# Reordering one step of a cross-attention block: seven-product sums between two transposes, low exponentials and the first norm ahead of the key copies

## The chip, the core and the metric

The kernel runs on one core of one Trainium2 chip. The metric is the time of one execution on the device in microseconds; the median of three runs stands for a kernel. A profiled execution gives in addition a trace of every engine, from which all rows in this document are copied.

The core has a matrix engine (TensorE, PE in the rows; its weight loads are PEld), a vector engine (VectorE, DVE), a scalar engine (ScalarE, ACT), a general engine (GpSimd, POOL) and SyncE (SP), whose queue only starts transfers here. Each engine carries out its own instructions in the order in which they were written, and waits on semaphores for the others.

## The reference

128 independent sequences of 128 positions with 256 features go through one block of cross-attention and a feed-forward network, all in float32:

```python
q = heads(x @ Wq + bq); k = heads(ctx @ Wk + bk); v = heads(ctx @ Wv + bv)   # 16 heads of 16
scores = where(j < i, q @ k.T / sqrt(16), -1e30)                            # strictly causal
attn = softmax(scores); attn[:, :, 0, :] = 0
x1 = layer_norm(x + (attn @ v) @ Wo + bo, ln1_g, ln1_b)
out = layer_norm(x1 + relu(x1 @ W1 + b1) @ W2 + b2, ln2_g, ln2_b)           # W1: 256 x 1024
```

## The kernel before

Two sequences make a pair, and 64 pairs `p` go through a software pipeline. From pair 5 on, one call `step(p)` does one turn of it: it works on five pairs at once, each in another stage. The first five pairs have functions of their own, and so have the last two (`behind`). The queues of all five engines are put under a manual schedule: an engine's order is the order of the calls in the code, and this order, written by hand, is what the change touches.

What one `step(p)` holds, by stages:

- **Attention weights of pair p.** `scores_both` computes the scores on TensorE into PSUM banks 0 to 3 (the high 64 rows of queries, 128 keys, "high") and 4 to 7 (the low 64 rows, 64 keys, "low"). VectorE adds the causal mask (line 378 for low, line 729 for high) and takes negative maxima (lines 733, 740). ScalarE makes the exponentials head by head with the maximum as bias (`exponential_by_head`, line 748: 16 instructions for high, reading PSUM, 16 for low, reading the masked copy in SBUF). VectorE sums them and takes the reciprocal (`sums`, lines 409 and 410, twice for high and once for low), and GpSimd scales by it (line 411). VectorE transposes the result in blocks of 32 (`turn`, line 424, three times), and SyncE brings the blocks to their partitions with 16 transfers (`bring`, line 439) as `pT`.
- **Projections.** Queries and keys of pair p + 1 and values of pair p, on TensorE (lines 257 and 289), copied out of PSUM by ScalarE (`queries` 268, `keys` 279, `values_out` 299 and 304). Tokens and context of pair p + 2 are transposed by VectorE (`tokens`, line 243). `keys` uses bank 0, `queries` bank 4, `values` bank 1.
- **Attention output of pair p - 2.** `weigh` multiplies `pT` by the values (lines 471 and 481) into bank 7, `context` copies it (493, ScalarE), `attention_out` applies Wo (500, bank 5), VectorE adds the input and takes statistics (526, 513, 514), GpSimd turns them into a scale and a shift (520, 521, 565), ScalarE applies them (`norm1`, line 542, two instructions), which gives `x1`. `turn_x1` transposes it: VectorE in blocks (651), then SyncE out to DRAM and back (lines 235 and 238, five transfers).
- **Feed-forward layer of pairs p - 3 and p - 4.** `hidden(p - 3)` multiplies by W1 (line 687, 32 matmuls in banks 2, 3, 4, 0) with ScalarE's ReLU behind it (693, eight instructions). `second_by_seven(p - 4)` does the product with W2 as seven products of half size (line 780) into bank 6 (`py`) and bank 7 (`pz`), from sums of `hT` that GpSimd makes (`combine_hidden`, 766 to 769). `sum_of_seven(p - 4)` puts the seven together with `x1b`, in five adds on VectorE (four of line 808 and one of line 816) into `t2`, followed by statistics (513, 514).
- **End of pair p - 5.** `norm2` on ScalarE (line 579, two instructions), `finish` on GpSimd (585, 586), `store` on SyncE (594). `residual1(p - 3)` on GpSimd (554, 557) makes `x1b` from `x1`.

Tiles are reused in turn: `t2` has two buffers, `x1`, `t1`, `x1T` two, `hT` and `hS` one; scores, their transposes and `pT` share four ("wide"). The whole order of TensorE in a step is `weigh`, scores, queries, `attention_out`, keys, values, the seven products, `hidden`.

Of the kernel before, what the change touches and what calls it, by code (L numbers as in the profile page):

```python
# [19 lines left out]
def tile_cross_attention_block(  # L20
# [26 lines left out]
    H = 16  # L47
# [225 lines left out]
    def keys(p):  # L273
        st = states[p]
        st["kT"] = proj.tile([P, KC, 2, TP], F32, tag="kT", name=f"kT_{p}")
        pk = project(wk, st["cT"], at_bank(0, f"pk_{p}") if p > 3 else bank(f"pk_{p}"))
        for m in range(KC):
            for e in range(2):
                nc.scalar.activation(  # L279
                    st["kT"][:, m, e, :], pk[:, m * TP : (m + 1) * TP], AF.Identity,  # L280
                    bias=bkh[:, m, e : e + 1], scale=half[:, e : e + 1],
                )

    def values(p):
        st = states[p]
        pv = st["pv"] = at_bank(1, f"pv_{p}") if p > 3 else bank(f"pv_{p}")
        for s in range(2):
            for k in range(KC):
                nc.tensor.matmul(  # L289
                    pv[:, s * D : (s + 1) * D], st["cT"][:, k, s * P : (s + 1) * P], wv[:, k, :],  # L290
                    start=(k == 0), stop=(k == KC - 1),
                )

    def values_out(p):
        st = states[p]
        pv = st.pop("pv")
        st["vz"], st["vd"] = vzs[p % 2], vds[p % 2]
        for s in range(2):
            nc.scalar.copy(  # L299
                st["vz"][:, s, :, 0:4:3, :],  # L300
                pv[:, s * D : (s + 1) * D].rearrange("p (r e d) -> p r e d", e=2, d=DK),
            )
        for e in range(2):
            nc.scalar.copy(  # L304
                st["vd"][e * HP : (e + 1) * HP, :, :, e, :].rearrange("p s r d -> p (s r) d"),
                pv[:HP].rearrange("p (u e d) -> p u e d", e=2, d=DK)[:, :, e, :],
            )
# [93 lines left out]
    def sums(p, hi, part):  # L401

        st = states[p]
        sm = st["sm", hi]
        n = sm.shape[2]
        su = small.tile([P, H], F32, tag=f"su{hi}", name=f"su{hi}_{p}_{part.start}")
        rs = small.tile([P, H], F32, tag=f"rs{hi}", name=f"rs{hi}_{p}_{part.start}")
        su, rs = su[:, part], rs[:, part]
        nc.vector.tensor_reduce(su, sm[:, part, :], AX.X, ALU.add)  # L409
        nc.vector.reciprocal(rs, su)  # L410
        nc.gpsimd.tensor_tensor(  # L411
            sm[:, part, :], sm[:, part, :],
            rs[:, :, None].to_broadcast([P, part.stop - part.start, n]), ALU.mult,
        )
# [119 lines left out]
    def norm1(p):  # L534

        st = states[p]
        x1 = st["x1"] = ffn.tile([P, 2, D], F32, tag="x1", name=f"x1_{p}")
        t1, mv, sd = st.pop("t1"), st.pop(("mv", 1)), st.pop(("sd", 1))
        for s in range(2):
            if p != 1:  # L540

                nc.scalar.activation(  # L542
                    x1[:, s], t1[:, s], AF.Identity, bias=st["nb", 1][:, s], scale=sd[:, s]
                )
                continue
            nc.vector.tensor_scalar(
                x1[:, s], t1[:, s], mv[:, s, 0:1], sd[:, s], ALU.subtract, ALU.mult
            )

    def residual1(p):  # L550

        st = states[p]
        x1b = st["x1b"] = ffn.tile([P, 2, D], F32, tag="x1b", name=f"x1b_{p}", bufs=3)
        nc.gpsimd.tensor_tensor(
            x1b, st["x1"], g1_r[:, None, :].to_broadcast([P, 2, D]), ALU.mult
        )
        nc.gpsimd.tensor_tensor(
            x1b, x1b, be1b_r[:, None, :].to_broadcast([P, 2, D]), ALU.add
        )

    def shift(p, i):
        st = states[p]
        nb = st["nb", i] = small.tile([P, 2, 1], F32, tag=f"nb{i}", name=f"nb{i}_{p}")
        for s in range(2):
            nc.gpsimd.tensor_scalar(
                nb[:, s], st["mv", i][:, s, 0:1], st["sd", i][:, s], -1.0, ALU.mult, ALU.mult
            )
# [7 lines left out]
    def norm2(p):  # L575
        st = states[p]
        t2, sd, nb = st["t2"], st["sd", 2], st["nb", 2]
        for s in range(2):
            nc.scalar.activation(  # L579
                t2[:, s], t2[:, s], AF.Identity, bias=nb[:, s], scale=sd[:, s]  # L580
            )
# [160 lines left out]
    def exponential_by_head(p, hi, heads):  # L742

        st = states[p]
        sm, nmx = st["sm", hi], st["nmx", hi]
        for h in heads:
            src = st["sps", 1][h // 4][:, h % 4 * P : h % 4 * P + P] if hi else sm[:, h, :]
            nc.scalar.activation(sm[:, h, :], src, AF.Exp, bias=nmx[:, h : h + 1], scale=1.0)  # L748
# [359 lines left out]
    def step(p):  # L1108
        last = p == NP - 1
        weigh(p - 2)  # L1110
        context(p - 2)
        scores_both(p)
        if p > 6:
            combine_hidden(p - 4, POOL_ALONE)
        if p == 5:
            second_sum(1)
            finish(0)
            store(0)
        add_bo(p - 1)
        load_ahead(p)  # L1120
        mask(p, 0, B)
        mask_high(p, A)
        exponential_by_head(p, 1, ONES)
        mask_high(p, B)
        exponential_by_head(p, 1, TWOS)
        mask(p, 0, A)
        low_maximum(p)
        if p > 5:
            norm2(p - 5)
        if not last:  # L1130
            queries(p + 1)
        exponential_by_head(p, 0, range(H))
        attention_out(p - 2)
        attention_sum(p - 2)
        attention_stats(p - 2)
        shift(p - 2, 1)
        if not last:
            keys(p + 1)
        values(p)
        values_out(p)  # L1140
        sums(p, 1, ONE)
        sums(p, 1, TWO)
        sums(p, 0, ALL)
        residual1(p - 3)
        if p > 6:
            second_by_seven(p - 4)
        elif p == 6:
            second_half(2, 1)
        norm1(p - 2)
        hidden(p - 3, range(FC // 2 if p == 5 else 0, FC))  # L1150
        if p == 5:
            second_half(2, 0)
        if p + 2 < NP:
            tokens(p + 2, "x")
            tokens(p + 2, "c")
        turn_x1(p - 2)
        turn(p, 1, 0)
        turn(p, 1, 1)
        turn(p, 0, 0)
        bring(p, nc.sync, LATE_FIRST)  # L1160
        if p > 5:
            finish(p - 5)
            store(p - 5)
        if p > 6:
            sum_of_seven(p - 4)
        stats(p - 4, states[p - 4]["t2"], 2)
        scale_and_shift(p - 4)

# [3 lines left out]
    for p in range(5, NP):  # L1172
        step(p)
# [23 lines left out]
    p = NP - 1  # L1197
# [71 lines left out]
```

## Time and profile before

| | |
|---|---|
| median of three runs | 1646.58 us (1645.24 to 1646.58) |
| the profiled execution's own time | 1644.42 us |
| its span, first to last instruction | 1642.4 us |
| granted TensorE clock, mean | 0.996 |
| TensorE, VectorE, GpSimd, ScalarE busy | 93%, 82%, 77%, 68% |
| DMA engines busy, data moved | 53%, 204.21 MB |

How to read it: rows of the waits name the waiting engine, the tile and line, then whom it waited for, the microseconds in total, how many times, and the longest. Rows of the timeline begin with the start and the length in microseconds, then engine, line, operation, what it writes and reads, and how many instructions are merged in the row; in brackets stands the engine's idle time just before it and what ended it. "issue" there is waiting for nothing that the profile shows. SPq is SyncE's queue of transfers, and the length of such a row is the time of issuing, not of moving.

### The profile page before, as it was taken

To read this page: it belongs to the slowest core of one execution; us is meant where nothing else is said; L and a number is where in the kernel's file an instruction comes from. 1 tells how busy PE (TensorE), PEld (TensorE's weight loads), DVE (VectorE), ACT (ScalarE), POOL (GpSimd) and SP (SyncE) were. 2 spreads that over 40 slices of the span, in tenths; PEclk is the share of its full clock that TensorE was granted. 3 is DMA by queue.
4 is the path that set the end of the run, shared out by engine and by line. 5 is a ranking of instruction groups with operands and counts; after the bars stand their busy time and mean duration, and the time that the engine had idled before them with its cause. 6 is when DMAs were issued, how large, how long until landed. Compare 5 with 4: busy or idle time off the path is not lost.

```text
span 1642.4 us, 47426 instructions
## 1 busy us (share of the span) xinstructions
PE 1526.3 (93%) x17926; PEld 1362.6 (83%) x17926; DVE 1347.6 (82%) x2490; ACT 1116.4 (68%) x3391; POOL 1265.9 (77%) x1290
## 2 busy tenths in 40 slices
PE   8998999999999999999999999999999999999998
PEld 7777888888888888888888888888888888888887
DVE  7978888888888888888888888888888888888764
ACT  5666676676776766766767767667667677676652
POOL 7876787787777877877877778778778778787774
PEclk9999999999999999999999999999999999999999
DMA  8454555555555555555555655555555555554331
GB/s 187 91 133 117 139 125 141 122 130 120 124 138 126 120 130 124 125 141 121 130 121 125 137 124 122 132 121 126 144 121 128 123 123 136 128 119 121 94 97 45
DMA packets 415283, 204.21 MB, mean 124 GB/s; under 512 B 282448, under 2 KB 383056, under 8 KB 415056
## 3 DMA queue, kind: packets, MB, share of 16 engines
q1 hardware_dynamic: 413152, 200.13, 52.0%
q8 instruction: 142, 2.33, 0.6%
q10 hardware_dynamic: 1904, 1.06, 0.3%
q14 instruction: 85, 0.70, 0.1%
HBM read 70.26 MB, written 33.29 MB: 63 GB/s over the span
## 4 chain that ended last, share of the span: by engine, by line
ACT 44%; DVE 25%; PE 18%; issue 7%; DMA 2%; SPq 2%; POOL 2%; DVEq 0%; ACTq 0%; POOLq 0%
ACT sm L748 25%; DVE tb L424 12%; DVE t L808 6%; ACT kT L279 6%; ACT x L542 4%; ACT t L579 3%; PE ph L687 3%; PE pss L364 3%; PE pc L481 3%; ACT qT L268 2%; PE pc L471 2%; DVE pss L729 2%; ACT vd L304 2%; SPq L439 2%; ACT vz L299 2%
## 5 line engine op out<-in xcount | busy, mean ns | idle before, releaser
L687 PE MATMUL ph<-x1T,w 128*128 128x256 f32 x2048 | 453.8, 379 | 3.1 <-ACT kT L279 3.1
L687 PEld LDWEIGHTS ph<-x1T,w 128*128 128x128 f32 x2048 | 384.5, 190 | 53.9 <-ACT kT L279 3.5
L411 POOL TENSOR_TENSOR sm<-sm,rs 128x1024 f32<-128x1024 f32 x192 | 359.5, 1900 | 2.7 <-DVE rs L410 2.2
L693 ACT ACTIVATE hT<-ph,b1e_c 128x256 f32<-128x256 f32 x504 | 211.3, 471 | 204.3 <-PE ph L687 192.9
L748 ACT ACTIVATE sm<-pss,nmx 128x128 f32<-128x128 f32 x944 | 250.5, 415 | 130.5 <-DVE nmx L733 87.7
L409 DVE TENSOR_REDUCE su<-sm 128x8 f32<-128x1024 f32 (+1 forms) x192 | 228.8, 1192 | 61.0 <-ACT sm L748 57.1
L520 POOL TENSOR_SCALAR ve<-mv 128x2 f32<-128x2 f32 x127 | 29.5, 233 | 307.3 <-DVE mv L514 297.0
L748 ACT ACTIVATE sm<-sm,nmx 128x64 f32<-128x64 f32 x944 | 236.0, 443 | 0.0
L424 DVE STREAM_TRANSPOSE tb<-sm 128x1024 f32<-128x1024 f32 x186 | 214.4, 1202 | 0.0
L780 PE MATMUL py<-wt,hS 128*128 128x128 f32 x1440 | 172.2, 276 | 3.1 <-POOL hS L767 3.1
L780 PEld LDWEIGHTS py<-wt,hS 128*128 128x128 f32 x1440 | 166.5, 193 | 3.7 <-POOL hS L767 3.7
L378 DVE TENSOR_TENSOR sm<-pss,neg 128x256 f32<-128x256 f32 (+1 forms) x276 | 108.0, 433 | 67.8 <-PE pss L364 65.3
L733 DVE TENSOR_REDUCE nmx<-pss 128x4 f32<-128x512 f32 x236 | 150.6, 678 | 0.0
L471 PE MATMUL pc<-pT,vd 128*32 128x64 f32 x2048 | 53.8, 222 | 83.0 <-DVE t L816 81.0
L257 PE MATMUL pq<-xT,wq 128*128 128x256 f32 x504 | 126.9, 395 | 4.2 <-DVE sm L378 4.2
L279 ACT ACTIVATE kT<-pk,bkh,half 128x256 f32<-128x256 f32 x252 | 125.9, 639 | 4.0 <-PE pk L257 4.0
L493 ACT COPY cxT<-pc 128x508 f32<-128x508 f32 x64 | 37.3, 582 | 132.6 <-PE pc L481 119.0
L471 PEld LDWEIGHTS pc<-pT,vd 128*32 128x32 f32 x2048 | 36.5, 109 | 107.9 <-DVE t L816 103.7
L289 PE MATMUL pv<-wv,cT 128*128 128x256 f32 x512 | 121.1, 379 | 1.6 <-ACT sm L748 1.6
L500 PE MATMUL po<-wo,cxT 128*128 128x256 f32 x512 | 121.2, 379 | 0.0
L257 PE MATMUL pk<-cT,wk 128*128 128x256 f32 x504 | 119.2, 379 | 0.0
L364 PE MATMUL pss<-kT,qT 32*64 32x256 f32 (+1 forms) x3840 | 103.8, 330 | 10.9 <-issue 10.3
(131 smaller groups left out, 3155.9 us busy)
## 6 DMA issues: line engine op xcount, KB each, us to landing
pT<-tb SPq DMA_DIRECT2D x984, 96.0 KB
x1t<-tbx SPq DMA_DIRECT2D x252, 64.0 KB
x1T<-x1t SPq DMA_DIRECT2D x63, 256.0 KB
out_dram<-t SPq DMA_DIRECT2D x63, 256.0 KB
xb<-in_x_dram SPq DMA_DIRECT2D x124, 128.0 KB
cb<-in_ctx_dram SPq DMA_DIRECT2D x124, 128.0 KB
x<-in_x_dram SPq DMA_DIRECT2D x31, 512.0 KB
w<-in_L_xattn_W_dram SPq DMA_DIRECT2D x2, 1024.0 KB
```

Of the source, the lines that this page charges most:

```text
L257: nc.tensor.matmul(ps[:, m * TP : (m + 1) * TP], w[:, k, m * P : (m + 1) * P], src[:, k, :], start=(k == 0), stop=(k == KC - 1),)
L279: nc.scalar.activation(st["kT"][:, m, e, :], pk[:, m * TP : (m + 1) * TP], AF.Identity, bias=bkh[:, m, e : e + 1], scale=half[:, e : e + 1],)
L364: nc.tensor.matmul(st["sps", hi][r][s * HP : (s + 1) * HP, m * 2 * n : (m + 1) * 2 * n].rearrange("p (e j) -> p e j", e=2), st["qT"][strip ...
L409: nc.vector.tensor_reduce(su, sm[:, part, :], AX.X, ALU.add)
L411: nc.gpsimd.tensor_tensor(sm[:, part, :], sm[:, part, :], rs[:, :, None].to_broadcast([P, part.stop - part.start, n]), ALU.mult,)
L424: nc.vector.transpose(st["tb"][:, :, at : at + 256].rearrange("p j (n a) -> p n j a", a=32), st["sm", hi].rearrange("p h j -> p (h j)")[:, ...
L471: nc.tensor.matmul(pc[32 * j : 32 * j + 32, at : at + HP], st["vd"][:, s, 4 * m + j].rearrange("p e d -> p (e d)"), pT[:, 2 * s : 2 * s + ...
L687: nc.tensor.matmul(ph[:, i * TP : (i + 1) * TP].rearrange("p (s i a) -> p s i a", s=2, a=32), w1[:, k, (f + i) * P : (f + i + 1) * P], st[ ...
L693: nc.scalar.activation(st["hT"][:, f + i, :], ph[:, i * TP : (i + 1) * TP], AF.Relu, bias=(b1e_c if p else b1_c)[:, f + i : f + i + 1], sc ...
L733: nc.vector.tensor_reduce(st["nmx", 1][:, 4 * r : 4 * r + 4], st["sps", 1][r].rearrange("p (n j) -> p n j", j=P), AX.X, ALU.max, negate=True,)
L748: nc.scalar.activation(sm[:, h, :], src, AF.Exp, bias=nmx[:, h : h + 1], scale=1.0)
L780: nc.tensor.matmul(out, left(k), right(k), start=(k == 0), stop=(k == FC // 2 - 1))
```

## The change

Only the order of calls in `step` changes; every instruction stays.

- VectorE: `turn_x1` goes ahead of `tokens` (and, in steps 5 and 6, of the sums in `second_half`); `sum_of_seven` goes from behind all three `turn` calls to behind the first of them. The statistics of `t2` stay at the end.
- ScalarE, from step 6 on: before, the order was high exponentials, `norm2`, queries, low exponentials, keys, values, `norm1`. Now it is high exponentials, low exponentials, queries, `norm1`, keys, values, `norm2`. In step 5, which has no `norm2`, the low exponentials come behind `norm1` and keys.
- TensorE, GpSimd and SyncE keep their own order.

```diff
         low_maximum(p)
         if p > 5:
-            norm2(p - 5)
+            exponential_by_head(p, 0, range(H))
         if not last:
             queries(p + 1)
-        exponential_by_head(p, 0, range(H))
         attention_out(p - 2)
         attention_sum(p - 2)
         attention_stats(p - 2)
         shift(p - 2, 1)
+        norm1(p - 2)
         if not last:
             keys(p + 1)
+        if p == 5:
+            exponential_by_head(p, 0, range(H))
         values(p)
         values_out(p)
+        if p > 5:
+            norm2(p - 5)
         sums(p, 1, ONE)
         sums(p, 1, TWO)
         sums(p, 0, ALL)
+        turn_x1(p - 2)
         residual1(p - 3)
         if p > 6:
             second_by_seven(p - 4)
         elif p == 6:
             second_half(2, 1)
-        norm1(p - 2)
         hidden(p - 3, range(FC // 2 if p == 5 else 0, FC))
         if p == 5:
             second_half(2, 0)
         if p + 2 < NP:
             tokens(p + 2, "x")
             tokens(p + 2, "c")
-        turn_x1(p - 2)
         turn(p, 1, 0)
+        if p > 6:
+            sum_of_seven(p - 4)
         turn(p, 1, 1)
         turn(p, 0, 0)
         bring(p, nc.sync, LATE_FIRST)
         if p > 5:
             finish(p - 5)
             store(p - 5)
-        if p > 6:
-            sum_of_seven(p - 4)
         stats(p - 4, states[p - 4]["t2"], 2)
         scale_and_shift(p - 4)
```

## The prediction

> **What bounds the kernel now.** I read the busy shares first, then who waits for whom, then the timelines of one middle step engine by engine.
>
> ```profile
> PE 1526.3 (93%) x17926; PEld 1362.6 (83%) x17926; DVE 1347.6 (82%) x2490; ACT 1116.4 (68%) x3391; POOL 1265.9 (77%) x1290
> ```
> ```profile
> PE pc L471 <- DVE t L816: 81.0, 53, 2.0
> ...
> PE pss L364 <- issue: 10.3, 12, 1.4
> ```
> TensorE is busy 93% of the span, and of its 116 us of idle time 81.0 us are one wait: `weigh` (line 471), which opens each step, waits for line 816, the last of the five adds of `sum_of_seven`. Both use PSUM bank 7: `weigh` writes it, the adds read `pz` out of it. The timeline of TensorE shows a step of the steady state, and then the seventh step and the last of the 56 like it:
>
> ```profile
> 827.96 0.43 PE L471 MATMUL pc<-pT,vd 128*32 128x64 f32 x16 [0.42 <-DVE t L816]
> ...
> 843.35 1.06 PE L780 MATMUL pz<-w,hS 128*128 128x128 f32 x8
> 844.24 7.07 PE L687 MATMUL ph<-x1T,w 128*128 128x256 f32 x32
> 853.02 0.43 PE L471 MATMUL pc<-pT,vd 128*32 128x64 f32 x16 [1.71 <-DVE t L816]
> ```
> ```profile
> 143.86 7.07 PE L687 MATMUL ph<-x1T,w 128*128 128x256 f32 x32
> 150.86 0.43 PE L471 MATMUL pc<-pT,vd 128*32 128x64 f32 x16
> ...
> 1555.46 0.43 PE L471 MATMUL pc<-pT,vd 128*32 128x64 f32 x16 [1.74 <-DVE t L816]
> ```
> I call the start of line 471 T. A step takes 853.02 - 827.96 = 25.06 us, and from 150.86 to 1555.46 there are 56 of this length. Its matmuls reach line 687 at T+16.28 (844.24). Where nothing is waited for, line 471 follows line 687's start after 7.00 us (143.86 to 150.86), so TensorE alone needs **23.28 us** per step: 1.78 us less than it takes, 0.07 more than the listed 1.71.
>
> Why the adds are late is read from VectorE and ScalarE in the same step:
>
> ```profile
> 830.24 0.76 DVE L378 TENSOR_TENSOR sm<-pss,neg 128x256 f32<-128x256 f32 x2 [1.13 <-PE pss L364]
> ...
> 835.40 1.22 DVE L740 TENSOR_REDUCE nmx<-sm 128x16 f32<-128x1024 f32 x1
> ...
> 840.89 0.20 DVE L410 RECIPROCAL rs<-su 128x8 f32<-128x8 f32 x1
> 842.09 1.22 DVE L409 TENSOR_REDUCE su<-sm 128x16 f32<-128x1024 f32 x1 [1.00 <-ACT sm L748]
> ...
> 843.51 0.65 DVE L243 STREAM_TRANSPOSE xT<-xb 128x512 f32<-128x512 f32 x1
> ...
> 846.15 0.71 DVE L651 STREAM_TRANSPOSE tbx<-x 128x512 f32<-128x512 f32 x1 [1.40 <-ACT x L542]
> 846.79 3.46 DVE L424 STREAM_TRANSPOSE tb<-sm 128x1024 f32<-128x1024 f32 x3
> 850.17 0.65 DVE L808 TENSOR_TENSOR t<-x1b,py 128x512 f32<-128x512 f32 x1
> ...
> 852.41 0.55 DVE L816 TENSOR_TENSOR t<-t,pz 128x384 f32<-128x384 f32 x1
> ...
> 853.99 0.18 DVE L514 BATCH_NORM_AGGREGATE mv<-bs 128x2 f32<-128x6 f32 x1
> ```
> ```profile
> 832.34 4.25 ACT L748 ACTIVATE sm<-pss,nmx 128x128 f32<-128x128 f32 x16 [2.13 <-DMA pT<-tb]
> 836.35 1.21 ACT L579 ACTIVATE t<-t,nb,sd 128x256 f32<-128x256 f32 x2
> 837.34 0.95 ACT L268 ACTIVATE qT<-pq,bqs_c 128x256 f32<-128x256 f32 x2
> 838.05 4.00 ACT L748 ACTIVATE sm<-sm,nmx 128x64 f32<-128x64 f32 x16
> 841.87 2.01 ACT L279 ACTIVATE kT<-pk,bkh,half 128x256 f32<-128x256 f32 x4
> ...
> 845.03 1.09 ACT L542 ACTIVATE x<-t,nb,sd 128x256 f32<-128x256 f32 x2
> ```
> So the loop that sets 25.06 us is: ScalarE from its first exponential to `norm1` (832.34 to 846.12), VectorE's transpose of x1, three transposes and five adds (846.15 to 852.96), TensorE's line 471 and the scores, VectorE's first maxima, ScalarE again. VectorE stands still for 1.00 + 1.40 us in it while `sum_of_seven`'s inputs lie ready: the last product ends at 843.35 + 1.06 = 844.41, 5.8 us before the first add.
>
> **The change part by part.** No instruction is added or removed. I lay the new order out from T with start-to-start times of the rows above.
>
> ScalarE. The low exponentials start when line 740 is done (835.40 + 1.22 = T+8.7, a bubble of 0.3 us, since the first sixteen end at 836.35), take 3.82 us (838.05 to 841.87) and end at T+12.5 in place of T+13.9. `qT` takes 0.71 and ends at T+13.2; its readers are the next step's scores. `norm1` takes 1.09 and ends at **T+14.3** in place of T+18.2; its scale must be there:
>
> ```profile
> 839.63 0.50 POOL L565 TENSOR_SCALAR nb<-mv,sd 128x1 f32<-128x1 f32 x2
> 840.09 5.61 POOL L411 TENSOR_TENSOR sm<-sm,rs 128x1024 f32<-128x1024 f32 x3
> ```
> It is, at T+12.2. `kT` and the copies of the values 3.16 (841.87 to 845.03) and `norm2` 0.99 bring ScalarE to T+18.5, against T+18.2 now. The first `hT` behind it thus slips by 0.3 us. Its cover is line 687's own length: the last `hT` waits for the last of its matmuls at T+23.3 in any case, so this costs nothing; without that cover it costs 0.3 us a step.
>
> VectorE. Up to the second reciprocal nothing moves (840.89 + 0.20 = T+13.1). The third sum no longer waits: with its reciprocal 1.42, to T+14.55. The x1 transpose follows without a wait (0.64, T+15.2), then the two of x and c (1.24, T+16.45), then one `tb` transpose (3.38 / 3 = 1.13, T+17.6; the weights it reads are scaled by T+14.0, a third of line 411). The adds find the products ready (T+16.45) and take 2.79 (850.17 to 852.96): bank 7 is free at **T+20.4**, 2.9 us before TensorE wants it at T+23.28. Then two transposes (2.25, T+22.7; scaled by T+17.7) and the statistics (852.96 to 854.17, 1.21, T+23.9). The next step's first mask cannot come before 2.28 us after its own T (830.24), that is T+25.56: VectorE has some 1.6 us to spare.
>
> What is late next is nothing on this list: TensorE. So each of the 53 waits goes, with the 0.07 us beside it: 81.0 + 53 x 0.07 = **84.7 us**. The steps with less than 1.71 us of wait are those in which TensorE had already lost time to "issue" in the scores; that loss stays and is in the sum, since only the wait that was left is taken off.
>
> SyncE's queue keeps its order, but what it issues is to run in 23.28 us:
>
> ```profile
> 825.45 11.55 SPq L439 DMA_DIRECT2D pT<-tb  x16
> 837.10 0.53 SPq L594 DMA_DIRECT2D out_dram<-t  x1
> 837.68 3.04 SPq L92 DMA_DIRECT2D xb<-in_x_dram  x4
> 846.89 1.79 SPq L235 DMA_DIRECT2D x1t<-tbx  x4
> 850.18 0.38 SPq L238 DMA_DIRECT2D x1T<-x1t  x1
> ```
> 11.55 + 0.53 + 3.04 + 1.79 + 0.38 and 1.5 for the landing that line 238 waits for are 18.8 us. The five transfers of `turn_x1` (lines 235 and 238) keep their place behind the loads, which end at T+12.8 (840.72) here; their data is ready at T+15.2 in place of T+18.9. The 16 `pT` transfers start behind the third transpose, T+22.7, and are read a whole step later: hidden.
>
> GpSimd. `norm2` now ends at T+18.5 in place of T+9.4; its reader, `finish`, stands behind line 411, which ends at T+17.7 (845.70), and the two instructions of `residual1`: hidden too.
>
> Step 5 is ordered on its own: there `norm1` and `kT` come ahead of the low exponentials.
>
> ```profile
> 115.83 0.50 POOL L565 TENSOR_SCALAR nb<-mv,sd 128x1 f32<-128x1 f32 x2
> ...
> 121.22 1.54 ACT L693 ACTIVATE hT<-ph,b1e_c 128x256 f32<-128x256 f32 x4
> ...
> 124.68 0.42 DVE L831 TENSOR_TENSOR t<-py,x1b 128x256 f32<-128x256 f32 x1 [5.88 <-PE py L825]
> ```
> `norm1` waits for its scale to 116.3, is done at 117.4, `kT` at 119.2, the low exponentials at 123.0, the copies at 124.4 (all with the lengths above): `hT` starts there in place of 121.22. TensorE's product behind it and line 831 come some 1.9 us later; the x1 transpose (0.64) now stands ahead of line 831, so 1.2 us are lost, once. Bounds: 0 to 1.9.
>
> Unknown is one cost: **new "issue" stalls.** The twelve stand in the scores, by turns four and five steps apart, as the first three show (1.17 us with 17 of 64 matmuls to go, 0.67 with 3 to go, then with 18). TensorE's instructions come in blocks:
>
> ```profile
> 255.34 0.67 PE L364 MATMUL pss<-kT,qT 32*64 32x256 f32 x17 [1.17 <-issue]
> ...
> 355.24 0.43 PE L364 MATMUL pss<-kT,qT 32*64 32x128 f32 x3 [0.67 <-issue]
> ...
> 480.72 0.67 PE L364 MATMUL pss<-kT,qT 32*64 32x256 f32 x18 [0.82 <-issue]
> ```
> ```profile
> q8 instruction: 142, 2.33, 0.6%
> ```
> 2.33 MB in 142 packets are 16 KB each, some 2.2 per step, and a block border wanders through the step; I take it that the stall is a block that comes late when two borders fall within line 471 and the scores. The wait at line 471 gave a border just ahead of it 1.7 us of cover, and that is gone. The pattern repeats in nine steps, so I estimate that one step in nine has a border there, 6 in all. Each costs between nothing and 1.78 us: 0 to 10.7, and the other way the twelve may shrink: at most their 12 x 1.4 = 17 us. I take 0.7 each, **+4.2**, nearest to the mean listed stall of 10.3 / 12 = 0.86. The Trainium skill ("Runtime: NRT & Kernel Launch", Instruction fetch mechanics) has fetches in blocks of 16 KiB, 256 instructions, as here, and calls the cost of a border mostly hidden; by that the term is 0 and the time 4 us lower. The 12 rows of "issue" speak for the larger value.
>
> The sum, against the profiled execution: span 1642.4 - 84.7 + 1.2 + 4.2 = 1563.1. That execution took 1644.42, 2.0 more than its span, and the median of the runs, 1646.58, is 2.2 above that: **1567 us**.
>
> **The rivals.**
>
> *SyncE becomes the bound.* Its 18.8 us go up to 21 in steps that also load tokens; if closer packing stretches them by 15%, a step takes 24.0 to 24.2. For it: it is the queue with most to issue after the change. Against: it stood idle before line 235 in most steps. Price: about 0.8 x 56 steps = 45 us given back, 1612.
>
> *A store holds the adds: slower.* `t2` has two buffers. The adds of one step write where the output lay that was normalised in the step before, and its store is issued behind the 16 `pT` transfers, some 11.9 us after they begin. A loop closes: `pT` issues and store (12.0) - landing L - adds (2.79) - two transposes (2.25) - next `pT` issues: 17.1 + L. It decides from L = 6.2 us (23.28), and makes the kernel slower from L = 8.0. The trace bounds L from above only by 13.1 (store at 837.10, adds at 850.17 unhindered); at that a step takes 30.2 us, 56 x 5.1 = 286 more: 1930. Against: the same 256 KB of `x1t` land within 850.18 - 846.89 = 3.3 us.
>
> *An "issue" stall in every step*, since no step pauses any more: 1.78 in each of the 44 steps that have none, 78 us, and 1641. Against: the seventh step (T = 150.86) followed on its predecessor without a pause, and has none.
>
> *The order written does not become the order run*: no change, 1646. All five engines are put under a manual schedule, and the rows above follow the code's order one by one.
>
> **How the numbers follow.** The forecast 0.80, with its own range from 1555 (no new stall, half of the old ones gone) to 1577 (10.7 and 1.9); SyncE 0.10; the store 0.05; stalls everywhere 0.03; not reordered 0.02. From 1555 to 1590 lie the forecast and the milder part of the SyncE case, some 8 in 10. Differences under 0.2% (3.3 us) can't be told from none here. Faster is the forecast, SyncE and the stalls, 0.93; same 0.02; slower 0.05.
>
> **What would show it.** In the changed profile the wait of line 471 for line 816 is gone or nearly so, T to T is 23.28 us, and line 816 ends some 2.9 us before line 471 starts. Lines 409 and 651 no longer wait for ScalarE; what is left of VectorE's idle time, 1.13 + 1.00 + 1.40 - 1.78 = 1.75 us a step, stands before line 378. "Issue" in the scores appears 12 to 18 times. The step after step 5 starts about a microsecond later. It is wrong if TensorE's line 471 waits for another line (808, 424), if line 808 waits for a DMA (the store), or if line 439 starts later from step to step (SyncE).

## The result and the profile after

| | before | after |
|---|---|---|
| median | 1646.43 us (1645.24 to 1646.58) | **1554.66 us** (1552.53 to 1555.99) |
| span of the profiled execution | 1642.4 us | 1554.0 us |
| granted TensorE clock, mean | 0.996 | 0.995 |

The ratio is **0.9443, 95% interval 0.9426 to 0.9459**: 92 us faster. The forecast was 1567 with 1555 to 1590 as its range; the time lies 12 us under the forecast and 0.3 us under the range's lower end.

The page of the changed kernel, busy shares and then the chain of work that ended last, by engine:

```profile
PE 1521.2 (98%) x17926; PEld 1363.3 (88%) x17926; DVE 1327.8 (85%) x2490; ACT 1120.5 (72%) x3391; POOL 1265.7 (81%) x1290
...
PE 92%; DVE 3%; POOL 3%; issue 1%; ACT 1%; DMA 0%; POOLq 0%; DVEq 0%
```

TensorE goes from 93% of the span to 98%, and 92% of the chain is now TensorE alone. The waits of the changed kernel (engine, tile and line, whom it waited for, total us, count, longest):

```profile
DVE sm L378 <- PE pss L364: 125.2, 57, 3.8
...
PE pss L364 <- issue: 5.4, 7, 1.3
...
DVE t L808 <- DMA out_dram<-t: 2.4, 1, 2.4
```

TensorE's wait at line 471 for line 816, 81.0 us before, has no row any more. VectorE's waits for ScalarE's exponentials and for x1, 57.1 and 83.0 us, are down to one of 5.6 us and one of 1.3 us; VectorE now waits for TensorE, ahead of the first mask. The "issue" rows of the scores have become *fewer*, 7 in place of 12. Line 808, which opens the adds, waits for a store once, in the last steps (until 1504.49 us); none of the 56 steps below has such a wait. One middle step of the changed kernel, T = 812.74, in the timelines of TensorE, VectorE, ScalarE and SyncE's queue:

```profile
812.74 0.43 PE L471 MATMUL pc<-pT,vd 128*32 128x64 f32 x16
...
829.04 7.07 PE L687 MATMUL ph<-x1T,w 128*128 128x256 f32 x32
836.04 0.43 PE L471 MATMUL pc<-pT,vd 128*32 128x64 f32 x16
```
```profile
815.04 0.76 DVE L378 TENSOR_TENSOR sm<-pss,neg 128x256 f32<-128x256 f32 x2 [2.13 <-PE pss L364]
...
825.80 1.17 DVE L409 TENSOR_REDUCE su<-sm 128x16 f32<-128x1024 f32 x1
...
827.17 0.66 DVE L651 STREAM_TRANSPOSE tbx<-x 128x512 f32<-128x512 f32 x1
...
830.07 0.65 DVE L808 TENSOR_TENSOR t<-x1b,py 128x512 f32<-128x512 f32 x1
...
832.31 0.55 DVE L816 TENSOR_TENSOR t<-t,pz 128x384 f32<-128x384 f32 x1
...
836.02 0.18 DVE L514 BATCH_NORM_AGGREGATE mv<-bs 128x2 f32<-128x6 f32 x1
```
```profile
826.00 1.08 ACT L542 ACTIVATE x<-t,nb,sd 128x256 f32<-128x256 f32 x2
...
831.07 0.81 ACT L693 ACTIVATE hT<-ph,b1e_c 128x256 f32<-128x256 f32 x2
```
```profile
835.18 12.40 SPq L439 DMA_DIRECT2D pT<-tb  x16
...
854.99 0.38 SPq L238 DMA_DIRECT2D x1T<-x1t  x1
```

The step takes 836.04 - 812.74 = 23.30 us, without a wait in it. The adds end at 832.86, 3.2 us before TensorE's next line 471. Line 409 and line 651 start without a pause, and the first `norm1` starts at T+13.3 and the pair ends at T+14.3. SyncE works from 835.18 to 855.37, 20.2 us of 23.3 with its pauses for landings, and stays ahead. The first and last of the 56 steps that the prediction counted:

```profile
156.52 0.43 PE L471 MATMUL pc<-pT,vd 128*32 128x64 f32 x16
...
1467.64 0.43 PE L471 MATMUL pc<-pT,vd 128*32 128x64 f32 x16
```

56 steps in 1311.1 us. Fifty of them take 23.29 us, give or take 0.04; the other six hold what is left of the "issue" stalls. The first of the six, in TensorE's timeline of the changed kernel:

```profile
342.85 0.43 PE L471 MATMUL pc<-pT,vd 128*32 128x64 f32 x16
...
347.23 0.43 PE L364 MATMUL pss<-kT,qT 32*64 32x128 f32 x3 [1.33 <-issue]
...
367.85 0.43 PE L471 MATMUL pc<-pT,vd 128*32 128x64 f32 x16
```

It takes 25.00 us. The six begin at 342.85, 554.18, 764.87, 975.79, 1186.13 and 1397.05, nine steps apart, all with 3 to 6 of the 64 matmuls of the scores to go, and lose 6.7 us together (25.00 + 24.29 + 24.58 + 24.01 + 24.59 + 24.01, less 6 x 23.29). Before, there were twelve: six at the same place and six with 17 to 20 matmuls to go. Those are gone.

**Where forecast and trace part.** The forecast was a span of 1563.1, the trace has 1554.0. Three differences make up the 9.1 us:

| part | before | forecast | after |
|---|---|---|---|
| start to line 471 of the seventh step | 150.86 | 152.1 | 156.52 (4.5 slower) |
| the 56 steps | 1404.6 | 1324.1 | 1311.1 (13.0 faster) |
| from there to the end | 86.9 | 86.9 | 86.4 (0.6 faster) |

From the span to the median the forecast added 4.2 us, as before (1646.58 - 1642.4). Here it was 0.7 (1554.66 - 1554.0), 3.5 us less: the profiled execution of before, 1644.42 us, was faster than all four runs of before in the table, and that of the changed kernel, 1555.99 us, the slowest of its four. So the main term came out, and two terms of the span were wrong with opposite signs; which executions were profiled did the rest. The experiments are about these two, and about which half of the change carries the gain.

### The profile page after: what moved, and what is told of

It is laid out like the page before. It is cut to its first block, busy times and chain, and to the rows that moved or that the text cites. A ratio compares the mean times of both kernels' runs of the same rounds, so it can differ in the third digit from the quotient of the medians.

```text
span 1554.0 us, 47426 instructions
## 1 busy us (share of the span) xinstructions
PE 1521.2 (98%) x17926; PEld 1363.3 (88%) x17926; DVE 1327.8 (85%) x2490; ACT 1120.5 (72%) x3391; POOL 1265.7 (81%) x1290
## 4 chain that ended last, share of the span: by engine, by line
PE 92%; DVE 3%; POOL 3%; issue 1%; ACT 1%; DMA 0%; POOLq 0%; DVEq 0%
PE ph L687 27%; PE py L780 13%; PE pz L780 10%; PE pq L257 8%; PE po L500 7%; PE pv L289 7%; PE pk L257 7%; PE pss L364 6%; PE pc L481 3%; PE pc L471 2%; POOL sm L411 1%; PE py L705 0%; DVE tb L424 0%; DVE sm L378 0%; POOL sd L521 0%
## 5 line engine op out<-in xcount | busy, mean ns | idle before, releaser
L748 ACT ACTIVATE sm<-sm,nmx 128x64 f32<-128x64 f32 x944 | 231.9, 334 | 5.1
L424 DVE STREAM_TRANSPOSE tb<-sm 128x1024 f32<-128x1024 f32 x186 | 220.7, 1213 | 0.0
L279 ACT ACTIVATE kT<-pk,bkh,half 128x256 f32<-128x256 f32 x252 | 120.3, 558 | 4.0 <-PE pk L257 4.0
L257 PEld LDWEIGHTS pq<-xT,wq 128*128 128x128 f32 x504 | 91.7, 192 | 25.8 <-issue 9.4
L289 PEld LDWEIGHTS pv<-wv,cT 128*128 128x128 f32 x512 | 97.1, 190 | 15.1 <-ACT sm L748 2.0
L500 PEld LDWEIGHTS po<-wo,cxT 128*128 128x128 f32 x512 | 98.0, 192 | 14.0 <-ACT cxT L493 0.3
L257 PEld LDWEIGHTS pk<-cT,wk 128*128 128x128 f32 x504 | 95.7, 190 | 13.1 <-issue 0.2
```

The costliest lines, as they stand in the source:

```text
L257: nc.tensor.matmul(ps[:, m * TP : (m + 1) * TP], w[:, k, m * P : (m + 1) * P], src[:, k, :], start=(k == 0), stop=(k == KC - 1),)
L279: nc.scalar.activation(st["kT"][:, m, e, :], pk[:, m * TP : (m + 1) * TP], AF.Identity, bias=bkh[:, m, e : e + 1], scale=half[:, e : e + 1],)
L289: nc.tensor.matmul(pv[:, s * D : (s + 1) * D], st["cT"][:, k, s * P : (s + 1) * P], wv[:, k, :], start=(k == 0), stop=(k == KC - 1),)
L424: nc.vector.transpose(st["tb"][:, :, at : at + 256].rearrange("p j (n a) -> p n j a", a=32), st["sm", hi].rearrange("p h j -> p (h j)")[:, ...
L500: nc.tensor.matmul(po[:, s * D : (s + 1) * D], cxT[:, k, s, :], wo[:, k, :], start=(k == 0), stop=(k == KC - 1),)
```

## The experiments

The theories, by the names that the expectations use. **L (lead)**: the "issue" stall depends on how early line 471's wait is met. While TensorE stands at line 471, the blocks of instructions behind it come late; when the wait has been met some microseconds before, the near border is passed in time. **D (transfers)**: a block comes late because it meets SyncE's 16 `pT` transfers, and what the change altered is when these start against line 471 (2.5 us ahead before, 827.96 - 825.45; 0.9 us after, 836.04 - 835.18). **S**: the slower fill is the new order of step 5. All kernels run more than once were compared with the kernel before in runs on the same chip, whose medians there were 1647.45 to 1647.8.

### ScalarE's order and the early transpose of x1, without the adds' move

The changed kernel with the adds put back behind all three transposes; the early transpose of x1 stays.

```diff
         turn(p, 1, 0)
-        if p > 6:
-            sum_of_seven(p - 4)
         turn(p, 1, 1)
...
+        if p > 6:
+            sum_of_seven(p - 4)
         stats(p - 4, states[p - 4]["t2"], 2)
```

> The changed kernel with sum_of_seven put back behind all three turn calls; ScalarE's new order and the early turn_x1 stay. Laid out by the changed kernel's rows (norm1 ends at T+14.3, the third sum waits for nothing), the adds end at about T+22.4, some 0.9 us before line 687 is through at T+23.29. Theory A (ScalarE's order and the earlier x1 transpose carry the gain, the move of the adds only adds margin): line 471 does not wait, a step takes 23.29 us, 1555 to 1560 us in all. Rival (both parts are needed): a step of 24 us or more, above 1590. On the issue stalls: theory L (TensorE's queue of instructions stands still at line 471's wait, so that the block border some 35 instructions behind it is met late; once the wait is met early, the queue runs ahead) expects that with 0.9 us of lead the stalls with 17 to 20 matmuls to go come back in part, 0.3 to 0.9 us each in about six steps, time 1557 to 1560; theory D (stalls depend on when the pT transfers run beside them; here these start some 2.8 us earlier against T than in the changed kernel, as in the kernel before) expects all twelve back at 1.0 to 1.8 us, 1563.

Measured: 1558.82 us (1556.37 to 1561.82), ratio 0.9462 (0.9445 to 0.9478). VectorE's last add in the middle step, the `pT` transfers, TensorE's line 471 behind them, and a stall in a later step:

```profile
835.02 0.55 DVE L816 TENSOR_TENSOR t<-t,pz 128x384 f32<-128x384 f32 x1
```
```profile
832.87 10.74 SPq L439 DMA_DIRECT2D pT<-tb  x16
```
```profile
836.49 0.43 PE L471 MATMUL pc<-pT,vd 128*32 128x64 f32 x16
...
1097.79 0.68 PE L364 MATMUL pss<-kT,qT 32*64 32x256 f32 x19 [0.37 <-issue]
```

ScalarE's order and the early transpose of x1 by themselves bring the whole step down to 23.29 us: the adds end at 835.57, still 0.92 us in time. Moving the adds widens this lead to 3.2 us; by the medians that is worth 4 us, by the ratios 3, but the intervals overlap. And the stalls with 17 to 20 matmuls to go come partly back: those six steps lose 0.06 to 0.96 us, 2.3 together. They lost 1.2 to 2.0 each where line 471 waited (before: the step's length less 23.28 and less what was left of the wait at the next line 471), and nothing with 3.2 us of lead (after). That is the order which L asks for. D does not give it: here `pT` starts earlier against line 471 than in either, 836.49 - 832.87 = 3.6 us ahead, and the loss is not the largest but between the two. The two parts of this kernel, ScalarE's order and the early transpose, were not run apart.

### The adds alone

The kernel before with the adds between the first and the second transpose, ScalarE's order untouched.

```diff
         turn(p, 1, 0)
+        if p > 6:
+            sum_of_seven(p - 4)
         turn(p, 1, 1)
...
-        if p > 6:
-            sum_of_seven(p - 4)
         stats(p - 4, states[p - 4]["t2"], 2)
```

> The kernel before with sum_of_seven moved between the first and the second turn call, nothing else. By the rows of before: norm1 ends at T+18.2, the x1 transpose at 18.8, the first tb transpose at 20.0, the adds at 22.75, 0.5 us before TensorE would want bank 7; the two transposes at 25.0, the statistics at 26.2, which is later than the first mask could start (T+25.56). Theory A: TensorE's wait at line 471 goes, but VectorE becomes the bound with 26.2 - 2.28 = 23.95 us a step, line 378 follows the statistics without a wait and line 257 or 364 shows small waits for line 378: 1646.4 - 56 x 1.11 = 1584, with the stalls up to 1592. Rival (the adds' place is the whole of the gain): 23.3 us a step, 1555 to 1562. Rival (no gain without ScalarE's order): 1640 or more.

Measured: 1587.42 us (1586.45 to 1588.69), ratio 0.9632 (0.9616 to 0.9649). Waits of this kernel:

```profile
DVE tbx L651 <- ACT x L542: 82.2, 59, 2.6
DVE su L409 <- ACT sm L748: 56.7, 58, 1.3
...
PE pq L257 <- DVE sm L378: 25.8, 38, 4.4
...
PE pss L364 <- issue: 9.3, 12, 1.2
```
```profile
826.82 0.43 PE L471 MATMUL pc<-pT,vd 128*32 128x64 f32 x16
...
850.83 0.43 PE L471 MATMUL pc<-pT,vd 128*32 128x64 f32 x16
```

TensorE's wait at line 471 is gone here too, but a new one stands in its place: line 257 waits for VectorE's first mask to free bank 4, and the step is 850.83 - 826.82 = 24.01 us. VectorE still stands its 1.4 + 1.0 us behind ScalarE in every step, so it is now the bound: its work and these two pauses fill the step. The two halves, alone worth 60 and 89 us, are worth 92 together: they shorten the same loop, and TensorE's 23.29 us are a floor under both. All twelve "issue" stalls are here, six of them with 17 to 20 matmuls to go: line 471 no longer waits, but the adds end only 0.26 us ahead of it, and `pT` starts 2.05 us behind it (828.87). So no standing wait is needed for these stalls, only too small a lead; and they come although the transfers start late, which D does not explain.

### Step 5 as before

The changed kernel with the order of calls before in step 5 alone.

```diff
-        norm1(p - 2)
+        if p > 5:
+            norm1(p - 2)
...
-        turn_x1(p - 2)
+        if p > 5:
+            turn_x1(p - 2)
```

In step 5 the low exponentials, `norm1` and `turn_x1` get their old places.

> The changed kernel with step 5 alone in the order of the kernel before (low exponentials ahead of keys, norm1 and turn_x1 in their old places); all later steps as changed. In the changed kernel line 471 of the seventh step starts at 156.5 us, before at 150.9. Theory S (step 5's late low exponentials hold back GpSimd's third scaling, so residual1's x1b, which line 831 waits for): the seventh step starts at 151 to 152, time 1549 to 1551. Rival (the loss comes from step 6's new order or from the run): it stays near 156 and the time at 1554.

Measured: 1551.96 us (1548.92 to 1553.56), ratio 0.9417 (0.9402 to 0.9433). The fill on TensorE, of the kernel before, of the changed one and of this one:

```profile
104.14 0.43 PE L471 MATMUL pc<-pT,vd 128*32 128x64 f32 x16
...
119.14 1.99 PE L687 MATMUL ph<-x1T,w 128*128 128x256 f32 x8 [3.07 <-ACT kT L279]
...
132.01 3.38 PE L257 MATMUL pq<-xT,wq 128*128 128x256 f32 x8 [4.21 <-DVE sm L378]
135.23 1.89 PE L500 MATMUL po<-wo,cxT 128*128 128x256 f32 x8
```
```profile
104.46 0.43 PE L471 MATMUL pc<-pT,vd 128*32 128x64 f32 x16
...
126.79 0.43 PE L471 MATMUL pc<-pT,vd 128*32 128x64 f32 x16
...
136.10 3.78 PE L257 MATMUL pq<-xT,wq 128*128 128x256 f32 x8 [4.91 <-DVE sm L378]
139.68 3.10 PE L500 MATMUL po<-wo,cxT 128*128 128x256 f32 x8
```
```profile
104.65 0.43 PE L471 MATMUL pc<-pT,vd 128*32 128x64 f32 x16
...
119.65 3.43 PE L687 MATMUL ph<-x1T,w 128*128 128x256 f32 x8 [3.07 <-ACT kT L279]
...
133.95 3.78 PE L257 MATMUL pq<-xT,wq 128*128 128x256 f32 x8 [4.39 <-DVE sm L378]
137.53 2.95 PE L500 MATMUL po<-wo,cxT 128*128 128x256 f32 x8
...
154.22 0.43 PE L471 MATMUL pc<-pT,vd 128*32 128x64 f32 x16
```

With the sixth step's line 471 at 124.52 (before), 126.79 (after) and 126.46 (here), the loss against before splits by stretches (one execution each):

| stretch | after | this kernel |
|---|---|---|
| start of step 5 | 0.32 | 0.51 |
| step 5 | 1.95 | 1.43 |
| step 6 up to line 257 | 1.82 | 0.00 |
| line 257 to the seventh step | 1.57 | 1.42 |
| sum | 5.66 | 3.36 |

The seventh step begins at 154.22, between the 151 to 152 of theory S and the 156 of its rival. So the order of step 5 costs 1.95 + 1.82 = 3.8 us in the changed kernel, of the 5.7; in place of that this kernel's execution lost 1.43 us in the same eight matmuls of line 687 (3.43 us against 1.99). By the medians of the runs the old order of step 5 gains 2.7 us. The 1.82 us come by GpSimd and VectorE of the changed kernel:

```profile
124.83 1.90 POOL L411 TENSOR_TENSOR sm<-sm,rs 128x1024 f32<-128x1024 f32 x1 [4.49 <-ACT hT L693]
...
128.06 1.27 POOL L557 TENSOR_TENSOR x1b<-x1b,be1b_r 128x512 f32<-128x512 f32 x1
```
```profile
129.37 0.42 DVE L831 TENSOR_TENSOR t<-py,x1b 128x256 f32<-128x256 f32 x1 [4.11 <-POOL x1b L557]
```

The late low exponentials make the third sum late and with it GpSimd's third scaling (an idle time of 4.49 us ahead of it). Behind that GpSimd makes `x1b`, and line 831 waits 4.11 us for it. VectorE's token transposes and turns queue behind line 831, the first mask of step 6 behind those, and line 257 behind the mask.

What differs from run to run is the clock. The windows behind the same gap of 3.07 us, of the kernel before and of this one (columns: us; busy PE, PEld, DVE, ACT, POOL; granted clock; DMA share; GB/s):

```profile
119.10:124.50 5.40, 5.36 (x24) 4.48 (x24) 0.00 (x0) 3.63 (x10) 5.28 (x4) 1.00 0.86 173
```
```profile
119.60:126.40 6.80, 6.75 (x24) 5.53 (x24) 0.00 (x0) 3.74 (x10) 5.30 (x4) 0.78 0.69 142
```

1.00 in one execution and 0.78 in the other, at the same code and the same gap. Behind the gap ahead of line 257 the changed kernel had 0.54:

```profile
136.00:142.60 6.60, 6.50 (x16) 5.21 (x17) 5.97 (x13) 4.79 (x19) 2.27 (x4) 0.54 0.63 151
```

There the eight matmuls of line 257 take 3.78 us and those of line 500 3.10, against 3.38 and 1.89 before; that makes the loss from line 257 on, 1.57 us. The kernel with the adds alone, whose step 5 is written as before too, reached its seventh step at 154.73. The traces' records of the granted clock show it at one half for 3.41 us between 100 and 150 us in before, for 6.83 us in the changed kernel and for 10.24 us in this one; the other traces of this document have 6.83 or 10.24 us there. A stretch of 3.41 us at half the clock loses 1.7 us of work. The profiled execution of before thus had the best clock of all in its fill, worth some 3 us against this kernel. The Trainium skill ("TensorE: Matmul & The Clock Gate", Part 1) explains such a spread by an activity window that runs freely and doesn't begin with the kernel; the two rows agree with that, and no run here shows the window itself.

### The block borders, moved by 57 instructions

57 empty instructions for TensorE, once, ahead of step 5. A step has 569 TensorE instructions by count in the built program, which is 2 x 256 + 57.

```diff
+    for _ in range(57):
+        nc.tensor.nop(hint="pad", nofuse=True)
     for p in range(5, NP):
         step(p)
```

> The changed kernel with 57 empty TensorE instructions once, ahead of step 5. A step has 569 instructions on TensorE, 57 more than two blocks of 256, so this moves the block borders against the steps by exactly one step. Theory B (an issue stall in the scores belongs to a block border): the stalls now at the steps starting at 342.9, 554.2, 764.9, 975.8, 1186.1 and 1397.1 us come one step earlier, at about 319, 530, 741, 952, 1162 and 1373 (each plus or minus the little that the start shifts), with the same number of matmuls to go (3 to 6). Rival (they belong to certain steps' work or transfers): they stay where they are. Time within 3 us of 1555 either way.

Measured, in one execution: 1557.44 us. The stalled steps begin at 320.76, 531.38, 742.29, 953.22, 1164.13 and 1375.03, with 3, 4, 4, 5, 5 and 6 matmuls to go: the same pattern, each exactly one step earlier. The first:

```profile
320.76 0.43 PE L471 MATMUL pc<-pT,vd 128*32 128x64 f32 x16
...
324.42 0.43 PE L364 MATMUL pss<-kT,qT 32*64 32x128 f32 x3 [0.62 <-issue]
```

The stalls follow the borders of 256 instructions, and not the number of the step, its work or its transfers. Counted in the program, a border lies 61 to 66 instructions behind the first of line 471 in the six steps that stall, and 33 to 38 behind it in the six that stalled only before (they come four steps earlier, and 4 x 569 is 28 short of 9 x 256); the next border, 256 later, then falls near the end of the scores or into them. Among the 56 steps those with a border at any other distance don't stall.

The traces also keep start and end of every packet of the instruction queue, the q8 of the prediction's row, one block of 16 KB each. For the six stalled steps of the changed kernel, in us behind T:

| step begins | packet starts | packet has landed | scores go on | step longer by |
|---|---|---|---|---|
| 342.85 | 1.4 | 2.9 | 4.4 | 1.7 |
| 554.18 | 1.1 | 2.3 | 3.7 | 1.0 |
| 764.87 | 1.1 | 2.5 | 4.0 | 1.3 |
| 975.79 | 1.1 | 2.2 | 3.4 | 0.7 |
| 1186.13 | 1.1 | 2.5 | 4.0 | 1.3 |
| 1397.05 | 1.1 | 2.1 | 3.4 | 0.7 |

The later the packet has landed, the longer the stall. In all 75 stalls in the scores that the nine traces with such stalls have from the seventh step on, the scores go on 1.1 to 1.7 us after a packet has landed. The profile ties no packet to an instruction; that these are the blocks waited for is read from the times.

### Borders out of the way, and borders in it

Seven empty TensorE instructions per step ahead of `hidden` make a step 576 long, 2.25 blocks, so that only four distances occur. 32 more, once, set them to 28, 92, 156 and 220; 61 set them to 63, 127, 191 and 255.

```diff
+        if p > 5:
+            for _ in range(7):
+                nc.tensor.nop(hint="pad", nofuse=True)
         hidden(p - 3, range(FC // 2 if p == 5 else 0, FC))
...
+    for _ in range(32):                      # 61 in the second kernel
+        nc.tensor.nop(hint="pad", nofuse=True)
     for p in range(5, NP):
```

> The changed kernel with 7 empty TensorE instructions in each step ahead of hidden, and 32 more once ahead of step 5. A step then has 576 instructions, 64 more than two blocks, so the border that falls behind the start of line 471 takes only four places, 28, 92, 156 and 220 instructions behind it (counted from the start of the program); in the changed kernel the stalls stood where it lay 61 to 66 behind. Theory B (the border's place decides): no issue stall in the scores, every step alike, and in all 6.9 us fewer lost to stalls, less what the 7 empty instructions cost per step (unknown: 23.29 us a step if they hide behind the seven products, up to 23.8 if each takes its own 60 ns). Time 1548 if they hide. Rival (stalls belong to steps or transfers): six stalls stay.

> The same 7 empty instructions per step as the run with a border at 28, 92, 156 and 220, but 61 in place of 32 ahead of step 5, which puts the border at 63, 127, 191 and 255: every fourth step has it inside 61 to 66. Theory B: an issue stall with 3 to 6 matmuls to go in every fourth step, 14 in all, each lengthening its step by 0.7 to 1.7 us (mean 1.1 in the changed kernel): 14 to 17 us more than the other padded kernel. Rival: no difference between the two.

Measured: with 32, 1548.92 us (1544.1 to 1550.73), ratio 0.9395 (0.9368 to 0.9423); with 61, 1563.5 us (1562.13 to 1564.84), ratio 0.949 (0.9471 to 0.9508). A step of the first in TensorE's timeline, and the waits of the second:

```profile
808.59 0.43 PE L471 MATMUL pc<-pT,vd 128*32 128x64 f32 x16
...
831.88 0.43 PE L471 MATMUL pc<-pT,vd 128*32 128x64 f32 x16
```
```profile
PE pss L364 <- issue: 12.0, 14, 1.3
```

With 32 there is no stall in any step, all are 23.28 to 23.30 us, and the empty instructions cost nothing that can be seen. With 61, 14 steps, every fourth, stall and take 23.81 to 24.89 us. The two kernels differ in nothing but the place of the borders, and by 14.6 us. One thing came out otherwise than expected: all 14 stalls stand at the last matmul of the scores, with 1 to go, where a border at 63 has 5 to go in the changed kernel. So the counted distances are not exact between kernels, by some eight instructions; that every fourth step stalls follows from the step's length alone.

### Transfers earlier, lead kept

The two transposes of tokens go behind the three turns from step 6 on, so that the 16 `pT` transfers start earlier against line 471.

```diff
-        if p + 2 < NP:
+        if p + 2 < NP and p == 5:
             tokens(p + 2, "x")
             tokens(p + 2, "c")
...
         turn(p, 0, 0)
+        if p + 2 < NP and p > 5:
+            tokens(p + 2, "x")
+            tokens(p + 2, "c")
         bring(p, nc.sync, LATE_FIRST)
```

> The changed kernel with the two tokens transposes behind the three turn calls from step 6 on. The adds end earlier still (at about T+18.9) and the pT transfers start 1.2 us earlier against T, near where they started in the kernel before (2.4 us ahead of line 471 there, 0.9 in the changed kernel, 2.1 here). Theory L (the stalls with 17 to 20 matmuls to go came from the queue standing at line 471's wait): they stay away, only those with 3 to 6 to go remain, six of them, 1553 to 1557. Theory D (they depend on the pT transfers running beside the scores): they come back, five or six more at 1.0 to 1.8 us, 1560 to 1564.

Measured, in one execution: 1552.22 us. SyncE's queue and TensorE:

```profile
830.61 11.79 SPq L439 DMA_DIRECT2D pT<-tb  x16
```
```profile
832.66 0.43 PE L471 MATMUL pc<-pT,vd 128*32 128x64 f32 x16
```

The transfers start 2.05 us ahead of line 471, nearly the 2.5 of the kernel before, and the stalls in the scores stay the seven of the changed kernel, 4.8 us in all against 5.4. D falls, L stands; the time is 0.8 us under what L gave. The packets of the instruction queue show the same, in the six steps with a border 33 to 38 instructions on:

| kernel | adds end ahead of T | `pT` starts | packet starts | stalls there |
|---|---|---|---|---|
| before | 0.06 us, waited for | 2.4 ahead of T | 1.3 to 2.0 behind T | 1.2 to 2.0 us lost |
| adds alone | 0.26 | 2.05 behind | 1.2 to 1.9 behind | rows of 0.5 to 1.1 us |
| without the adds' move | 0.92 | 3.6 ahead | 0.2 to 0.3 behind | 0.06 to 0.96 us lost |
| changed | 3.17 | 0.9 ahead | 1.0 to 1.6 ahead | none |
| this one | 4.36 | 2.05 ahead | 1.1 to 1.5 ahead | none |

With more lead the packet starts earlier and the stall goes; the start of `pT` has no such order. The borders 61 to 66 on are not reached by it: in all five kernels the packet of those steps starts 1.0 to 2.0 us behind T.

### The fill mended, and both together

Step 5 in its old order, and line 831 in it behind the three turns and their transfers, so that neither `x1b` nor `py` holds the transposes.

```diff
         hidden(p - 3, range(FC // 2 if p == 5 else 0, FC))
-        if p == 5:
-            second_half(2, 0)
...
         bring(p, nc.sync, LATE_FIRST)
+        if p == 5:
+            second_half(2, 0)
         if p > 5:
             finish(p - 5)
```

> The changed kernel with step 5 in the old order, and the add of second_half in step 5 (line 831) behind VectorE's transposes in place of ahead of them: VectorE had stood still 5.9 to 7.3 us before line 831, waiting for TensorE's product, with all transposes and then the next step's masks queued behind. Theory S: the masks of step 6 no longer come 5 us late, TensorE's wait before its queries (4.2 to 4.9 us) goes, and with it the low granted clock that followed these gaps (0.54 to 0.80): the seventh step starts near 148 us in place of 154 to 156, time 1545 to 1547. Rival (something else holds step 6): no gain over the run with step 5 as before, 1552.

Measured: 1545.1 us (1544.37 to 1546.59), ratio 0.9379 (0.9362 to 0.9397). The seventh step of TensorE begins at

```profile
146.64 0.43 PE L471 MATMUL pc<-pT,vd 128*32 128x64 f32 x16
```

and line 257's wait of 4.9 us is gone: 9.9 us earlier than in the changed kernel, of which 1.6 us come from an earlier start of step 5 (102.86 against 104.46), before anything differs between the two. The medians differ by 9.6 us. The last kernel adds the seven and the 32 empty instructions to this one.

> Both together: step 5 in the old order with line 831's add behind VectorE's transposes, and 7 empty TensorE instructions per step (32 once) that keep the block borders away from the scores. Theories B and S add: 9.6 us (the run with line 831 moved) and 5.7 us (the padded run) below the changed kernel's 1554.7: 1539, the seventh step starting near 148 us and every later step of 23.29 us up to the last. If the two gains were one and the same (a border in step 6 alone): 1545.

Measured in five rounds: **1539.27 us (1537.79 to 1541.65), ratio 0.9342 (0.9329 to 0.9355)**. It is the fastest of the kernels here, 15.4 us under the changed one, and 108 us under the kernel before; the two gains add up (9.6 + 5.7 = 15.3). Its seventh step begins at 148.37.

## Why the prediction was right, and where it was not

**The main step held.** The loop was named rightly, and its 84.7 us with it: the wait of line 471 is gone, a step is 23.29 us against 23.28, `norm1` ends at T+14.3 as laid out, the adds end at T+20.1 (20.4), the statistics at T+23.5 (23.9). VectorE's idle time ahead of line 378 is 2.13 us (1.75). `hT` starts at T+18.3 and costs nothing. The experiments add what the prediction had not said: ScalarE's order and the early transpose of x1 suffice together, and the adds' new place is margin.

**The step on "issue" stalls failed, in its sign.** The prediction added 4.2 us; in the 56 steps the stalls fell by 8.8 us, from 16.2 (1404.6 - 84.7 - 56 x 23.28) to 7.4 (1311.1 - 56 x 23.28). This is the 13.0 us by which the steps were faster than forecast. The prediction took the stalls as blocks that come late, which the moved borders and the packets' times confirm. It then took the wait at line 471 as cover for a border near it, and added 4.2 us for new stalls. The runs show the reverse for the borders 33 to 38 instructions on: the loss is 1.2 to 2.0 us a step where line 471 waits, 0.4 on average where the wait was met 0.9 us before, and nothing at 3.2 us. A pause on a semaphore did not give these fetches time; it cost them time: their packets started 1.3 to 2.0 us behind T before, and 1.0 to 1.6 us ahead of it after. The stalls 61 to 66 instructions on stayed nearly as they were, 6.7 us after against some 7.4 before. "No new stall, half of the old ones gone" stood in the prediction as the lower end, and in the steps that case is what came. That the time met that end so closely is luck: the fill (4.5 us slower) and the choice of the profiled executions (3.5 us faster) nearly cancelled. The row by which the term was chosen, 10.3 us in 12 waits, said what a stall costs and nothing of how many there would be. The rule of the Trainium skill weighed there, that a border's cost is mostly hidden, fits the changed kernel better than the rows of before did, since of 56 steps six stall; but the kernel with 61 empty instructions shows 14 such borders that are not hidden, at about 1.0 us each (14.6 / 14). A term of 0, as by that rule, would still have been 8.8 us too high.

**The step on step 5 was too small.** It followed ScalarE and TensorE up to line 831 and put 1.2 us, with 1.9 as the upper bound. That part cost 1.95. It left out GpSimd, which makes `x1b` behind the scaling that waits for the late exponentials: 1.82 us more. The remaining 1.9 of the 5.7 are the clock after the gaps of the fill and 0.3 us of an earlier offset. They were in no term: the sum took over the fill of an execution with a good clock.

**Slips in the working.** The range's upper end, 1577, adds up to 1574.5 with its own terms (10.7 in place of 4.2, 1.9 in place of 1.2). In the rival on the store, it is issued 11.65 us behind the first `pT` transfer (837.10 - 825.45), not 11.9. Neither changes the forecast.

**The rivals.** SyncE takes 20.2 us of 23.3 in the rows shown, as the prediction feared, but doesn't set the step. In the 56 steps line 808 never waits for a store: in the step shown the issue of the store ends at 848.21 and the next adds start at 853.36 without a wait, so that it lands within 5.2 us, short of the 6.2 from which it would decide. The one wait of line 808 for a store, 2.4 us, comes in the last steps; it ends at 1504.49, 4.5 us after the store ahead of it began to be issued (1499.95). "Issue" in every step and "not reordered" are ruled out by the rows of the step.

**Open.** Why a lead of some 3 us takes a border 33 to 38 instructions on, but not one 61 to 66 on, was not found: a limit to how far TensorE's instructions are fetched ahead would do it, but no run varies that. With the border at the same place a stall costs 0.5 us in one step and 1.7 in another, in the order in which the packets land; why the packets start and last differently (0.9 to 1.8 us in the stalls) was not found.

## What to carry to other kernels

First find the loop that sets the step, then see which engine in it stands still while another's work could come first; putting the wanted result ahead on an engine with idle time (ScalarE), and the transpose that reads it, was worth 89 us here, and the rest of the loop's cuts overlap with it, since the bound engine's own time is a floor under all of them. Before pricing stalls of instruction supply, count where the 256-instruction borders fall against the fast stretch and whether the engine waits just ahead of them; here a few empty instructions moved the borders without lengthening the step. A step with an order of its own (here the fill) has to be followed on every engine, GpSimd too, and priced with a clock that may be low after each gap.

## What the runs showed of the hardware

- A stretch of 160 small matmuls (lines 471, 481 and 364, some 3.1 us, with their weight loads 320 instructions) outruns TensorE's instruction supply when block borders fall 61 to 66 instructions, as counted, behind its start: 0.5 to 1.7 us each. The stretch goes on 1.1 to 1.7 us after a 16 KB packet of the instruction queue has landed (75 stalls).
- Waiting on a semaphore at its start makes this worse: a border 33 to 38 instructions on costs 1.2 to 2.0 us behind a wait, and nothing when the wait was met 3.2 us before. The packet starts 1.3 to 2.0 us behind the stretch's first matmul in the one case, and 1.0 to 1.6 us ahead of it in the other.
- Seven empty TensorE instructions in a step of 569 didn't lengthen the step (23.29 us with and without them).
- Behind the same gap of 3.07 us the granted clock was 1.00 over the next 5.4 us in one run and 0.78 over 6.8 us in another; the same eight matmuls took 1.99 and 3.43 us.
